# A graph layer's last stage: part of the sum moved from VectorE to accumulating DMAs, one maximum per tile shared with ScalarE, stores cut smaller

## The chip, the cores and the metric

The kernel runs on one core of a Trainium2 chip. Its engines are TensorE (PE), VectorE (DVE), ScalarE (ACT), GpSimd (POOL) and SyncE (SP); 16 DMA engines move data between DRAM and the core's SBUF. Each engine takes its instructions in program order and waits on semaphores. SP and ACT issue plain DMAs on queues q1 and q10, POOL issues its DMAs on q0. The metric is the device time of one execution in microseconds (us), lower is better. L12 is line 12 of the kernel before, unless the kernel after is named.

## What is computed

The input has 6250 nodes of 128 channels and 206250 edges (100000 in both directions and one loop for each node), sorted by their destination (dst). The reference, cut:

```
h = maximum(layernorm(x), 0)
feat = concat([h[dst], h[src] - h[dst]])
msg = feat @ W.T + b
out = segment_max(msg, dst)
return x + where(isfinite(out), out, 0)
```

With W = [W1 | W2] the message is (W1 - W2) h[dst] + b + W2 h[src]. The first two terms are the same for all edges of a dst. So the kernel computes, for each node, A + b with A = (W1 - W2) h, and B = W2 h; the result is x + A + b + max over the node's sources of B.

## The kernel before, in words

**Lanes.** Each of the 128 partitions (lanes) owns 49 consecutive dsts (the last lane owns 27), and their run of the sorted edges.

**Start (0 to about 170 us).** The kernel loads x, makes A + b and B on TensorE, stores B to a DRAM table `Bt`, and forms x + A + b in a DRAM table `XA`: first a DRAM to DRAM copy of x (L457), then five pairs of DMAs of POOL that add A + b to it, `G_.dma_start(..., accum_op=ALU.add)` (L508). VectorE also finds pairs of edges that fit a one-hot form (one edge at most for each source lane, place and dst) and those that don't, the rest.

**The dense part (the pairs).** 13 tiles t of 10 lanes each (8 in the last; 490 or 392 dst columns) run over 25 pairs of source groups i. For each of the 325 pairs, TensorE spreads an index (L782, PSUM tile `z`), ScalarE turns it into a one-hot `oh` (L783), TensorE multiplies B by it into PSUM tile `ps`, two banks of 490 columns (L831), and VectorE takes the running maximum into `acc2`, 980 columns a pair (L842). The first pair of a tile starts `acc2`: a copy for the first tile (L837), for the others the maximum of `ps` with the self edges that lie in `acc`, broadcast to both halves (L840). A tile's last pair folds both halves of `acc2` into `acc` (L849). ScalarE works two one-hots ahead. In tiles 1 and 2 it also counts list ends (L854), once for each pair.

**The stream.** The rest of the edges are 414 steps: step k has one row of `Bt` for each lane, gathered by an indirect DMA of POOL (L77) into the tile `rows`, which holds five groups of eight steps. VectorE takes a running maximum along the steps (L228, "stream step"), restarting it where a lane passes to a new dst. SP stores each finished group of 8 to a DRAM table `M` (L232). A 415th step joins runs that cross lanes. The steps are laid evenly over the pairs up to the 280th: `steps_until(k)` is 415 times (k - 1) over 278. On VectorE they stand between the maxima, so that a stream step which waits for its gather holds all the maxima behind it.

**The last gathers.** After the last store to `M`, POOL gathers 49 rows from `M`, the last one of each dst (L77, `HX<-M,last_e` x9 and `rows<-M,last_e` x40), one gather for each place in the lane.

**The tail.** The dsts of a lane go in six groups: places 0 to 8 (held in `HX`), then 9 to 16, 17 to 24, 25 to 32, 33 to 40 and 41 to 48 (in buffers of `rows`). In steps of four places, TensorE turns `acc` (L906), VectorE takes the maximum with the gathered rows (L907) and adds x + A + b (L911) from SBUF. These sums were loaded from `XA` ahead: 28 places into the tile `xa` when tile 6 starts, the other 21 into `T` in the last tile (`load_xa`, L814). Each group is stored when it is whole: lanes 0 to 111 by SP and the rest by ACT (L916).

The order on each engine is the order in which the program is written; nothing reschedules it.

Of the kernel before, what the change touches and what calls it, by code (L numbers as in the profile page):

```python
# [8 lines left out]
F32 = mybir.dt.float32  # L9
# [6 lines left out]
ALU = mybir.AluOpType  # L16
# [3 lines left out]
P = 128  # L20
# [8 lines left out]
LD = 49  # L29
# [3 lines left out]
NS = 414  # L33
# [3 lines left out]
U = 8  # L37
# [14 lines left out]
def gnn_kernel(tc, x, src, dst, W, b, out):  # L52
    nc = tc.nc
    N, C = x.shape
# [6 lines left out]
    NG = -(-NSX // U)  # L61
    GQ = 10
    LASTD = N - (P - 1) * LD
# [9 lines left out]
    def at(ap, offset, pattern):  # L73
        return bass.AP(tensor=ap.tensor, offset=ap.offset + offset, ap=pattern)
# [5 lines left out]
    with ExitStack() as ctx:  # L80
# [20 lines left out]
        with ExitStack() as body:  # L101
# [118 lines left out]
            def stream_step():  # L220
                k = state["ran"]
                if k == NSX:
                    return
                state["ran"] = k + 1
                i, j = divmod(k, U)
                G = Gt[i]
                if state["prev"] is not None:
                    V.scalar_tensor_tensor(G[:, j], state["prev"], slim[:, k:k + 1], G[:, j],  # L228
                                           op0=ALU.min, op1=ALU.max)
                state["prev"] = G[:, j]  # L230
                if j == U - 1 or k == NS:
                    nc.sync.dma_start(M_v[:, 1 + i * U:2 + i * U + j], G[:, :j + 1])  # L232

            def more_rows(to):
                while True:
# [506 lines left out]
            with ExitStack() as main:  # L742
# [61 lines left out]
                xa0 = fin1.tile([P, XD, C], F32, name="xa")  # L804
                xa1 = t3f[:, :(LD - XD) * C].rearrange("p (d c) -> p d c", c=C)

                def xa_of(d0, d1):
                    return xa0[:, d0:d1] if d1 <= XD else xa1[:, d0 - XD:d1 - XD]

                def load_xa(d0, d1):  # L810
                    for e, d2, d3, p0, p1 in ((nc.sync, d0, min(d1, LASTD), 0, 112), (A_, d0, min(d1, LASTD), 112, P),
                                              (nc.sync, max(d0, LASTD), d1, 0, 112), (A_, max(d0, LASTD), d1, 112, P - 1)):
                        if d2 < d3:
                            e.dma_start(xa_of(d2, d3)[p0:p1],  # L814
                                        at(XA, (p0 * LD + d2) * C, [[LD * C, p1 - p0], [1, (d3 - d2) * C]]))
# [4 lines left out]
                for k, (t, i) in enumerate(pairs):  # L820
# [13 lines left out]
                        self_edges(i)  # L834
                    more_rows(min(state["ran"] + 1, steps_until(k)))
                    if k == 0:
                        V.tensor_copy(a, ps[:, :, :n])  # L837
                    elif i == 0:
                        o = acc[:, c0:c0 + n].rearrange("c (o n) -> c o n", o=1).to_broadcast([P, 2, n])
                        V.tensor_tensor(a, ps[:, :, :n], o, ALU.max)  # L840
                    else:
                        V.tensor_tensor(a, a, ps[:, :, :n], ALU.max)  # L842
                    more_rows(steps_until(k))
                    oh = nxt
                    if k == Q // 2 - 1:
                        V.tensor_tensor(acc[:, c0:c0 + n], acc[:, c0:c0 + n], acc2[:, 0, :n], ALU.max)
                        V.tensor_tensor(acc[:, c0:c0 + n], acc[:, c0:c0 + n], acc2[:, 1, :n], ALU.max)
                    elif i == Q - 2:
                        V.tensor_tensor(acc[:, c0:c0 + n], acc2[:, 0, :n], acc2[:, 1, :n], ALU.max)  # L849
# [49 lines left out]
                V.tensor_copy(bad, bsum)  # L899
                acc_v = acc[:, :P * LD].rearrange("c (p d) -> c d p", d=LD)  # L900
                for R, (d0, d1) in zip(Rg, groups):
                    for j0 in range(d0, d1, 4):
                        j1 = min(j0 + 4, d1)
                        p = ps_f.tile([P, 4, P], F32, name="pf")
                        for j in range(j0, j1):
                            T_.transpose(p[:, j - j0], acc_v[:, j], ident)  # L906
                        V.tensor_tensor(R[:, j0 - d0:j1 - d0], R[:, j0 - d0:j1 - d0], p[:, :j1 - j0], ALU.max)  # L907
# [5 lines left out]
                    for e, d2, d3, p0, p1 in ((nc.sync, d0, min(d1, LASTD), 0, 112), (A_, d0, min(d1, LASTD), 112, P),  # L913
                                              (nc.sync, max(d0, LASTD), d1, 0, 112), (A_, max(d0, LASTD), d1, 112, P - 1)):
                        if d2 < d3:
                            e.dma_start(at(out, (p0 * LD + d2) * C, [[LD * C, p1 - p0], [1, (d3 - d2) * C]]),  # L916
                                        R[p0:p1, d2 - d0:d3 - d0])
                mid.close()


# [72 lines left out]
```

## Time and profile before

| | us |
|---|---|
| three runs: median (lowest, highest) | 790.54 (787.14, 792.31) |
| the profiled execution | 786.79 |
| its span, first to last instruction | 784.6 |
| VectorE busy | 724.9 (92%) |
| TensorE busy | 652.1 (83%) |
| ScalarE busy | 527.9 (67%) |
| GpSimd busy | 497.4 (63%) |

The tiles of the dense part take about 46 us each from 227 to 690 us, tile 11 ends at 732 us and tile 12 at 760 us; the tail is what follows. A row of a timeline has the start in us, the duration, the engine (SPq and ACTq are DMA issues), the line, the operation, what it writes <- what it reads, how many instructions were merged, and in brackets how long the engine sat idle before it and what ended the idle time. A row of windows has the stretch and its length, then busy us and number of instructions of PE, PEld (weight loads), DVE, ACT and POOL, the granted TensorE clock, the mean busy share of the DMA engines and GB/s. A row of a DMA queue has packets, MB, and the time of its packets as a share of 16 engines over the window.

### The profile page before, as it was taken

The numbers are of one execution on the slowest core, as the hardware profiler recorded it, in microseconds if no ns is written. First come the engines' busy times: TensorE is split into PE (matmuls) and PEld (weight loads), VectorE is DVE, ScalarE is ACT, GpSimd is POOL, SyncE is SP. The second block draws the span as 40 slices with busy tenths as digits, with TensorE's granted clock in tenths as the row PEclk, the third lists the DMA queues.
The fourth block names the chain that finished last, engine by engine and source line by source line (L and its number), as shares of the span: only waits on it lengthen the run. The fifth ranks groups of instructions, "written<-read, shape, count | busy, mean of one in ns | idle before, by whom it ended". The sixth has DMA issues, their size and how long they took to land. (4 is left out here: it accounts for less than half of the span.)

```text
span 784.6 us, 11914 instructions
## 1 busy us (share of the span) xinstructions
PE 652.1 (83%) x3571; PEld 421.7 (54%) x3571; DVE 724.9 (92%) x1329; ACT 527.9 (67%) x1212; POOL 497.4 (63%) x533
## 2 busy tenths in 40 slices
PE   1499776369888998699999998999999899898992
PEld 0254566348765555456555555655555555555661
DVE  5898999779799998999999999999999999997986
ACT  2659598337789999567576666657666665757740
POOL 5300012577777777777777767777777777747770
PEclk9799999559999999899999999999999999999996
DMA  3735264312334233333333373333333333324225
GB/s 87 212 89 209 37 131 96 88 48 81 105 89 117 80 104 105 103 102 109 105 103 105 105 188 110 106 104 104 103 107 102 103 105 105 104 84 111 62 57 169
DMA packets 77153, 83.05 MB, mean 106 GB/s; under 512 B 11585, under 2 KB 66213, under 8 KB 76677
## 3 DMA queue, kind: packets, MB, share of 16 engines
q1 hardware_dynamic: 60284, 45.40, 20.2%
q0 software_dynamic: 16096, 36.02, 17.1%
q10 hardware_dynamic: 700, 0.78, 0.6%
q8 instruction: 30, 0.49, 0.2%
q14 instruction: 43, 0.35, 0.1%
HBM read 44.41 MB, written 40.90 MB: 109 GB/s over the span
## 5 line engine op out<-in xcount | busy, mean ns | idle before, releaser
L77 POOL DMA_INDIRECT rows<-Bt,lists x414 | 416.6, 1006 | 135.2 <-DMA rows<-Bt,lists 44.5
L783 ACT ACTIVATE oh<-z 126x490 fp32r<-126x490 f32 (+1 forms) x650 | 336.9, 576 | 159.0 <-PE z L782 149.6
L831 PE MATMUL ps<-oh,Bp 126*128 126x490 f32 (+1 forms) x1300 | 389.1, 422 | 23.8 <-DVE acc L842 17.8
L842 DVE TENSOR_TENSOR acc<-acc,ps 128x980 f32<-128x980 f32 (+1 forms) x312 | 359.2, 1151 | 24.1 <-PE ps L831 19.4
L831 PEld LDWEIGHTS ps<-oh,Bp 126*128 126x128 f32 x1300 | 234.8, 193 | 147.1 <-DVE acc L842 90.5
L782 PE MATMUL z<-Vb,Sel 128*128 128x490 f16 (+1 forms) x650 | 195.0, 378 | 14.7 <-ACT oh L783 8.5
L228 DVE SCALAR_TENSOR_TENSOR rows<-rows,lists 128x128 f32<-128x128 f32 x414 | 142.1, 343 | 1.3 <-DMA rows<-Bt,lists 0.3
L191 PEld LDWEIGHTS <-HX 128*128 128x128 bf16 x896 | 68.1, 159 | 53.7 <-issue 36.7
L191 PE MATMUL pv<-HX 128*128 128x28 bf16 (+1 forms) x826 | 73.8, 232 | 16.2 <-ACT Vb L201 16.2
L782 PEld LDWEIGHTS <-Sel 128*128 128x128 f16 x650 | 43.2, 104 | 56.2 <-issue 54.6
L508 POOL DMA_DIRECT2D XA<-HX x10 | 9.9, 1215 | 95.4 <-issue 69.4
L168 DVE TENSOR_TENSOR HX<-T,IQ 128x700 bf16<-128x700 bf16 x128 | 65.3, 514 | 0.0
L560 PE MATMUL dup<-rows,identb 128*128 128x512 bf16 (+1 forms) x176 | 41.5, 376 | 14.9 <-DVE rows L569 13.6
L77 POOL DMA_INDIRECT rows<-M,last_e x40 | 37.7, 943 | 12.2 <-issue 7.0
L560 PEld LDWEIGHTS <-identb 128*128 128x128 bf16 x176 | 18.0, 102 | 36.8 <-issue 23.0
L854 ACT ACTIVATE dump<-lists,nbias 128x512 bf16<-128x512 f32 x50 | 37.6, 752 | 0.1
L499 PE MATMUL pm<-whi,lhl 128*125 128x256 f32 x100 | 25.4, 286 | 0.0
L499 PE MATMUL pm<-wlo,lhl 128*125 128x256 f32 x100 | 25.4, 286 | 0.0
L569 DVE TENSOR_TENSOR rows<-KA,KB 128x1792 bf16<-128x1792 int16 x22 | 23.9, 1085 | 0.9 <-PE dup L560 0.9
L476 ACT ACTIVATE rows<-HX,nmr,rstd 125x128 f32<-125x128 f32 x50 | 22.8, 523 | 2.5 <-DVE rows L421 2.5
L175 DVE TENSOR_TENSOR HX<-HX,T 128x392 bf16<-128x392 bf16 x64 | 23.2, 363 | 0.3
L569 DVE TENSOR_TENSOR rows<-KA 128x1792 bf16<-128x1792 int16 x21 | 22.7, 1082 | 0.6 <-PE dup L560 0.6
(264 smaller groups left out, 548.8 us busy)
## 6 DMA issues: line engine op xcount, KB each, us to landing
M<-rows SPq DMA_DIRECT2D x51, 512.0 KB
rows<-Bt,lists POOLq DMA_INDIRECT x414
HX<-in_x SPq DMA_DIRECT2D x5, 560.0 KB
Bt<-acc SPq DMA_DIRECT2D x5, 560.0 KB
XA<-HX POOLq DMA_DIRECT2D x5, 560.0 KB
out_x<-rows SPq DMA_DIRECT2D x4, 448.0 KB
xa<-XA SPq DMA_DIRECT2D x1, 1512.0 KB
T<-XA SPq DMA_DIRECT2D x1, 1176.0 KB
```

The costliest lines, as they stand in the source:

```text
L77: G_.indirect_dma_start(out=o, out_offset=None, in_=table, in_offset=bass.IndirectOffsetOnAxis(ap=idx, axis=0))
L168: V.tensor_tensor(oh, over(TQ, z - a), iq, ALU.is_equal)
L191: T_.matmul(o2[:, :, lo:lo + w], OHQ[:, :, i], OHD[:, :, :, i], start=False, stop=True, skip_group_check=True)
L228: V.scalar_tensor_tensor(G[:, j], state["prev"], slim[:, k:k + 1], G[:, j], op0=ALU.min, op1=ALU.max)
L499: T_.matmul(st["pm"][:L, j], a, w, start=False, stop=True, skip_group_check=True)
L560: T_.matmul(dup[:, c0:c1], m, e[:, c0:c1], start=first, stop=last)
L569: V.tensor_tensor(e, KA[:, 64:], i1, ALU.is_equal)
L782: T_.matmul(z[:, :n], Sel[:, Q - 1 - i - j], Vb[t % 2][:, :n], start=True, stop=True)
L783: A_.activation(oh[:, :n], z[:L + 1, :n], AF.Relu)
L831: T_.matmul(ps[:, j, :n], Bp[:, e, i + j], oh[j][:, :n], start=e == 0, stop=e == 1)
L842: V.tensor_tensor(a, a, ps[:, :, :n], ALU.max)
L854: A_.activation(dump, sdl, AF.Sign, scale=2.0, bias=nbias[:, c:c + 1], accum_out=ends[:, c:c + 1])
```

## The change

Five edits:

1. The first pair of a tile: in the first tile ScalarE makes the copy of both halves; in the other twelve, ScalarE copies the second half of `ps` and VectorE takes the maximum with `acc` for the first half alone.
2. The last group of the stream (7 steps): a store of five steps goes out after the fifth, and the last store has two steps in place of seven.
3. Places 0 to 24 (`SUM` = 25) take x + A + b in the output: when tile 7 starts, SP copies these places from `XA` to the output (one DRAM to DRAM DMA, 128 x 3200 elements). In the tail VectorE only takes their maximum, and POOL adds it to the output, one accumulating DMA for each of the three groups.
4. `xa` is loaded for places 25 to 27 alone.
5. The other 24 places are stored after each step of four places, and the last four in two steps of two.

```diff
+                if i == NG - 1 and j == (NS % U) - 2:
+                    nc.sync.dma_start(M_v[:, 1 + i * U:2 + i * U + j], G[:, :j + 1])
+                elif k == NS:
+                    j0 = (NS % U) - 1
                 if j == U - 1 or k == NS:
-                    nc.sync.dma_start(M_v[:, 1 + i * U:2 + i * U + j], G[:, :j + 1])
+                    nc.sync.dma_start(M_v[:, 1 + i * U + j0:2 + i * U + j], G[:, j0:j + 1])
...
+                SUM = groups[2][1]
...
                     if k == 0:
-                        V.tensor_copy(a, ps[:, :, :n])
+                        A_.copy(a, ps[:, :, :n])
                     elif i == 0:
-                        o = acc[:, c0:c0 + n].rearrange("c (o n) -> c o n", o=1).to_broadcast([P, 2, n])
-                        V.tensor_tensor(a, ps[:, :, :n], o, ALU.max)
+                        A_.copy(acc2[:, 1, :n], ps[:, 1, :n])
+                        V.tensor_tensor(acc2[:, 0, :n], ps[:, 0, :n], acc[:, c0:c0 + n], ALU.max)
...
+                    if i == 0 and t == len(tiles) // 2 + 1:
+                        w = [[LD * C, P], [1, SUM * C]]
+                        nc.sync.dma_start(at(out, 0, w), at(XA, 0, w))
                     if i == 0 and t in (len(tiles) // 2, len(tiles) - 1):
-                        load_xa(*((0, XD) if t < len(tiles) - 1 else (XD, LD)))
+                        load_xa(*((SUM, XD) if t < len(tiles) - 1 else (XD, LD)))
...
                 for R, (d0, d1) in zip(Rg, groups):
-                    for j0 in range(d0, d1, 4):
-                        j1 = min(j0 + 4, d1)
+                    cuts = list(range(d0, d1, 4)) + [d1]
+                    if d1 == LD:
+                        cuts.insert(-1, d1 - 2)
+                    for j0, j1 in zip(cuts, cuts[1:]):
                         p = ps_f.tile([P, 4, P], F32, name="pf")
                         for j in range(j0, j1):
                             T_.transpose(p[:, j - j0], acc_v[:, j], ident)
                         V.tensor_tensor(R[:, j0 - d0:j1 - d0], R[:, j0 - d0:j1 - d0], p[:, :j1 - j0], ALU.max)
+                        if d1 <= SUM:
+                            continue
                         ...
-                    for e, d2, d3, p0, p1 in ((nc.sync, d0, min(d1, LASTD), 0, 112), ...
+                        for e, d2, d3, p0, p1 in ((nc.sync, j0, min(j1, LASTD), 0, 112), ...
...
+                    if d1 <= SUM:
+                        G_.dma_start(at(out, d0 * C, [[LD * C, P], [1, (d1 - d0) * C]]), R[:, :d1 - d0],
+                                     accum_op=ALU.add)
```

On POOL, at the end of the program before: the gathers of the stream, the gather that joins runs, the 49 last gathers, and then the program's end (`bad` is a flag for inputs that the plan can't hold).

```order
L77 DMA rows<-Bt,lists 128x128 x414
L77 DMA rows<-M,lists 128x128
L77 DMA HX<-M,last_e 128x128 x9
L77 DMA rows<-M,last_e 128x128 x40
L922 TENSOR_LOAD bad
```

The same place in the program after (its lines are later by 6 to 19 in this part; L935 is the accumulating DMA of groups 0 to 2):

```order
L77 DMA rows<-Bt,lists 128x128 x414
L77 DMA rows<-M,lists 128x128
L77 DMA HX<-M,last_e 128x128 x9
L77 DMA rows<-M,last_e 128x128 x40
L935 DMA out_x<-HX 128x1152
L935 DMA out_x<-rows 128x1024 x2
L941 TENSOR_LOAD bad
```

All three accumulating DMAs stand behind the last of the 49 gathers.

On SP, from the stream's stores to the last load of `XA`, before:

```order
L232 DMA M<-rows 128x8x128 x27
L814 DMA xa<-XA 112x3456
L814 DMA xa<-XA 112x128
L232 DMA M<-rows 128x8x128 x24
L232 DMA M<-rows 128x7x128
L814 DMA T_85<-XA 112x2688
```

After (L238 and L234 are the stores to `M`, L823 the loads, L861 the copy to the output):

```order
L238 DMA M<-rows 128x8x128 x27
L823 DMA xa<-XA 112x256
L823 DMA xa<-XA 112x128
L238 DMA M<-rows 128x8x128 x5
L861 DMA out_x<-XA 128x3200
L238 DMA M<-rows 128x8x128 x19
L234 DMA M<-rows 128x5x128
L238 DMA M<-rows 128x2x128
L823 DMA T_85<-XA 112x2688
```

The load of `xa` shrinks to three places, the copy to the output comes five groups later on the same queue, and the stream's last store is cut in two.

On VectorE, the end of the program before, its last three steps of four places:

```order
L907 TENSOR_TENSOR rows<-rows,pf 128x512
L911 TENSOR_TENSOR rows<-rows,T_85 127x512
L907 TENSOR_TENSOR rows<-rows,pf 128x512
L911 TENSOR_TENSOR rows<-rows,T_85 127x512
L907 TENSOR_TENSOR rows<-rows,pf 128x512
L911 TENSOR_TENSOR rows<-rows,T_85 127x512
```

The start of VectorE's tail after (L921 is the maximum):

```order
L921 TENSOR_TENSOR HX<-HX,pf 128x512 x2
L921 TENSOR_TENSOR HX<-HX,pf 128x128
L921 TENSOR_TENSOR rows<-rows,pf 128x512 x5
L927 TENSOR_TENSOR rows<-rows,xa 128x256
L927 TENSOR_TENSOR rows<-rows,xa 127x128
L927 TENSOR_TENSOR rows<-rows,T_85 127x128
```

For the first 25 places the seven additions between the maxima are gone (the fifth maximum of the row x5 is that of places 25 to 28); from place 25 on a maximum and its additions alternate as before.

More of the change, by code (lines that the diff above doesn't have):

```diff
@@ L912, in gnn_kernel @@
                                                     ALU.add)
[L913 to L917, printed above, removed]
+                        for e, d2, d3, p0, p1 in ((nc.sync, j0, min(j1, LASTD), 0, 112), (A_, j0, min(j1, LASTD), 112, P),
+                                                  (nc.sync, max(j0, LASTD), j1, 0, 112), (A_, max(j0, LASTD), j1, 112, P - 1)):
+                            if d2 < d3:
+                                e.dma_start(at(out, (p0 * LD + d2) * C, [[LD * C, p1 - p0], [1, (d3 - d2) * C]]),
+                                            R[p0:p1, d2 - d0:d3 - d0])
+                    if d1 <= SUM:
+                        G_.dma_start(at(out, d0 * C, [[LD * C, P], [1, (d1 - d0) * C]]), R[:, :d1 - d0],
+                                     accum_op=ALU.add)
                 mid.close()
```

6 lines of the change are left out of this document (4 added, 2 removed).

## The prediction

> **What bounds the kernel now.** I read the page first, then windows by tile, the waits of VectorE, the timeline at both ends of the stream, and the DMA view of the tail. From the page, the engines and the gathers:
>
> ```profile
> PE 652.1 (83%) x3571; PEld 421.7 (54%) x3571; DVE 724.9 (92%) x1329; ACT 527.9 (67%) x1212; POOL 497.4 (63%) x533
> L77 POOL DMA_INDIRECT rows<-Bt,lists x414 | 416.6, 1006 | 135.2 <-DMA rows<-Bt,lists 44.5
> ```
>
> VectorE seems to be the bound, and in a middle tile (window view) it is busy for 45.75 of 46 us:
>
> ```profile
> 412.00:458.00 46.00, 42.11 (x224) 25.28 (x223) 45.75 (x84) 30.91 (x63) 35.34 (x36) 1.00 0.36 101
> ```
>
> But look at POOL's 36 gathers there. One takes 0.94 us when nothing stretches it, and 0.30 us pass before the next. The page's row says that 414 of them are busy for 416.6 us and idle for 135.2 us; 414 x 0.30 is 124 us, and 7.06 of the rest is the wait before the first. So the gathers run back to back from 148.86 us to 694: POOL is full too, though its column says 63%. The timeline shows who is ahead. POOL, gathers number 0, 1, 403 and 414 (11 gathers, and 11 steps, stand between 403 and the end):
>
> ```profile
> 148.86 1.04 POOL L77 DMA_INDIRECT rows<-Bt,lists  x1 [7.06 <-DVE lists L671]
> 150.20 1.23 POOL L77 DMA_INDIRECT rows<-Bt,lists  x1 [0.30 <-issue]
> 679.95 1.23 POOL L77 DMA_INDIRECT rows<-Bt,lists  x1 [0.30 <-DVE acc L842]
> 693.97 1.06 POOL L77 DMA_INDIRECT rows<-M,lists  x1 [0.31 <-DVE HX L168]
> ```
>
> VectorE, the stream steps that use the last three of these, and step 412:
>
> ```profile
> 178.57 0.35 DVE L228 SCALAR_TENSOR_TENSOR rows<-rows,lists 128x128 f32<-128x128 f32 x1
> 684.36 0.35 DVE L228 SCALAR_TENSOR_TENSOR rows<-rows,lists 128x128 f32<-128x128 f32 x1 [0.33 <-DMA rows<-Bt,lists]
> 695.91 0.34 DVE L228 SCALAR_TENSOR_TENSOR rows<-rows,lists 128x128 f32<-128x128 f32 x1
> 698.61 0.34 DVE L228 SCALAR_TENSOR_TENSOR rows<-rows,lists 128x128 f32<-128x128 f32 x1
> ```
>
> A step follows its gather's start by 28.4 us at first, by 4.41 at number 403 and 4.64 at the last. At 403 VectorE waited 0.33 us for the data: 4.41 us is how long a gather takes to land there. So VectorE has used up the whole lead of the gathers just when the stream ends. What it saves before that point it will spend waiting for gathers. This is the main reading of my prediction.
>
> **The tail.** PE, VectorE, POOL and the last store (timeline), the tail's window, then the DMA queues of 740 to 785 us and the busy tenths of the DMA engines from 774 to 785 (40 slices of 0.275 us):
>
> ```profile
> 759.99 5.56 PE L906 MATMUL pf<-ident,acc 128*128 128x128 f32 x29 [0.39 <-DVE acc L849]
> 760.79 0.69 DVE L907 TENSOR_TENSOR HX<-HX,pf 128x512 f32<-128x512 f32 x1 [0.60 <-PE pf L906]
> 769.35 0.68 DVE L907 TENSOR_TENSOR rows<-rows,pf 128x512 f32<-128x512 f32 x1
> ...
> 763.98 0.94 POOL L77 DMA_INDIRECT rows<-M,last_e  x1 [0.30 <-issue]
> 777.56 0.32 SPq L916 DMA_DIRECT2D out_x<-rows  x1
> 759.40:779.00 19.60, 9.84 (x51) 7.53 (x51) 17.04 (x31) 0.00 (x0) 4.30 (x5) 0.73 0.58 169
> q1 hardware_dynamic: 896, 2.81, 18.9%
> q10 hardware_dynamic: 218, 0.39, 5.0%
> ...
> DMA  9310009986976223999587510000000000000000
> ```
>
> VectorE sets the tail: it works from 760.79 to 777.5, busy for 17.04 of 19.6 us, the last store goes out at 777.56, the DMA engines fall idle at 780.4 (slice 23), and 4.2 us of closing work end the span at 784.6. All stores together took (18.9% + 5.0%) x 45 = 10.8 us of all 16 engines for 3.2 MB, so DMA has room today (0.58 busy in the window).
>
> **Edit 1, the first pair.** A whole maximum occupies VectorE for 1.09 us from its start to the next, one of 490 columns for 0.63 (first and third row, each with the start of the next):
>
> ```profile
> 462.88 1.17 DVE L840 TENSOR_TENSOR acc<-ps,acc 128x980 f32<-128x980 f32 x1
> 463.97 0.34 DVE L228 SCALAR_TENSOR_TENSOR rows<-rows,lists 128x128 f32<-128x128 f32 x1
> 461.72 0.70 DVE L849 TENSOR_TENSOR acc<-acc 128x490 f32<-128x490 f32 x1
> 462.35 0.35 DVE L172 TENSOR_TENSOR HX<-T,IW 128x392 bf16<-128x392 bf16 x1
> 463.67 1.05 ACT L783 ACTIVATE oh<-z 126x490 fp32r<-126x490 f32 x2 [0.81 <-PE z L782]
> 273.00:320.00 47.00, 42.19 (x221) 25.98 (x219) 44.70 (x83) 45.26 (x111) 36.33 (x36) 0.96 0.38 107
> 732.00:759.40 27.40, 25.86 (x142) 18.32 (x142) 24.87 (x27) 20.38 (x46) 20.69 (x23) 1.00 0.22 59
> ```
>
> So 0.46 to 0.5 us saved per tile. ScalarE's copy has no row; its nearest is the one-hot of the same 490 columns out of PSUM, half of 1.05, 0.5 us. It fits into the 0.81 us in which ScalarE waits there. Queued behind it are the one-hots of the pair after the next, which have that slack. In tiles 1 and 2 ScalarE is full (45.26 of 47 us), so there the copy costs what VectorE gains, but the gathers' lead of some 30 us covers that. The first tile's copy gains nothing: VectorE waits for `ps` around it. In tiles 3 to 11 VectorE saves 9 x 0.5 = 4.5 us, all before the stream's end, and of this only what the gathers allow arrives: number 403 lands at 684.36 as before, and of the 14.25 us of VectorE's work from there to the last step tile 11's first pair saves 0.5. The stream's end gains **0.5 us** of 4.5. Tile 12 starts behind the stream; TensorE is even fuller there (25.86 of 27.4 us, VectorE 24.87), so I count half of 0.5, **0.25**.
>
> **Edits 3 and 4, the loads.** The only hole in POOL's gathers, and the load of `xa` that made it (SP's row), with the DMA engines full (1.03 in the window):
>
> ```profile
> 457.01 1.56 SPq L814 DMA_DIRECT2D xa<-XA  x2
> 469.05 0.94 POOL L77 DMA_INDIRECT rows<-Bt,lists  x1 [2.63 <-DVE rows L228]
> 464.00:468.00 4.00, 3.38 (x13) 1.78 (x14) 4.00 (x10) 2.27 (x6) 1.89 (x2) 1.00 1.03 183
> 66.00:70.00 4.00, 3.66 (x17) 1.53 (x17) 4.00 (x5) 3.71 (x20) 0.00 (x0) 1.00 0.60 248
> ```
>
> 2.63 - 0.30 = 2.3 us lost on POOL, and as POOL is full, lost at the end. The load shrinks from 28 places to 3, but a copy of 25 places (1.64 MB) runs in tile 7. The last row is the same kind of copy (x to `XA`): it kept the engines at 0.60. POOL wins 2.3 us if the copy makes no hole, and loses 2.3 or so if its hole is twice as deep. Between them I take half of the old hole, a gain of **1.2 us**. The copy also stands ahead of 19 stores to `M` on SP's queue; a store that lands late holds POOL only when its buffer is due again, four groups or some 40 us later, so I price that at nothing; without that cover it would be the copy's length, some 8 us. The stream then ends 0.5 + 1.2 = 1.7 us earlier.
>
> **Edit 2, the cut store.** POOL waited for the last store to `M`, issued at 699.0 (first row):
>
> ```profile
> L232 SPq DMA_DIRECT2D M<-rows x52: 359/360/382, 186.5 to 699.0; - x52
> 702.75 0.94 POOL L77 DMA_INDIRECT HX<-M,last_e  x1 [7.72 <-issue]
> DMA  0000799700000050040140130005004099699998
> ```
>
> The last row, 698 to 716 us in slices of 0.45, shows its 448 KB moving in four slices, 1.8 us. Two steps of seven need 0.5, if the first five have gone by then (they leave after step 412, 2.7 us ahead): **1.3 us**; at worst nothing. With it the last gather ends at 764.92 - 1.7 - 1.3 = 761.9.
>
> **Edits 3 and 5, the tail.** Seven additions go from VectorE's path. But TensorE turns a place in 5.56/29 = 0.19 us, so the eighth maximum, the first with additions, begins 25 x 0.19 = 4.8 us after the first instead of 8.6 (769.35): VectorE's path gains 3.8 us. What comes late instead is the DMA work. POOL can issue the first accumulating DMA only behind its last gather, at 762.2, and needs about 1.2 us for it (mean of L508 below): data flow from 763.4. Their price comes from `XA`'s own. In 96 to 110 us one such pair ran beside a plain store of the same 0.64 MB (DMA slices of 0.35 us, then the plain queue and POOL's); last, POOL's issues of them:
>
> ```profile
> DMA  0000000799799999499999954000000000000000
> q1 hardware_dynamic: 154, 0.64, 14.6%
> q0 software_dynamic: 160, 0.64, 28.3%
> ...
> L508 POOL DMA_DIRECT2D XA<-HX x10 | 9.9, 1215 | 95.4 <-issue 69.4
> ```
>
> Of all 16 engines the plain store takes 2.04 us, the accumulating one 3.96, and the slices show both one after the other, 6 us: they add up. 25 places are 1.64 MB: 10.1 us. The other 24 places are 24/49 of 10.8, 5.3 us. That is 15.4 us of full DMA from 763.4 on: **778.8**, where it was 780.4. VectorE (last store at 777.56 - 3.8 - 1.95 = 771.8) no longer decides.
>
> The Trainium skill (DMA: Bandwidth & Descriptors, Anatomy of one DMA — SWDGE) fits a POOL DMA as 2.0 us and bytes over 436 GB/s. By that the three would move in 3.8 us, an estimate, and VectorE's path would stay the bound, as in rival B below. The trace disagrees for accumulating ones (3.96 us for 0.64 MB).
>
> **Sum.** 780.4 - 778.8 = 1.6 us off the span of 784.6. The profiled execution, 786.79, lies 3.75 us below the median; I take the same 1.6 off the median: **788.9 us**.
>
> **Rivals.** A, the gathers don't hold VectorE back (they land sooner than at 403): then 4.5 + 0.25 arrive. POOL's chain gains 4.5 + 1.3, DMA ends at 776.0: -4.4, 786.1 us. For it: number 403 was stretched (1.23 us where 0.94 is usual). Against it stands the wait at 684.36. B, accumulating DMAs hide among the stores, so that VectorE's path ends the tail: 771.8 + 2.8 (777.56 to 780.4), -5.8, 784.7 us. For it: today's tail leaves the engines at 0.58 on average. Against it: the sum of 2.04 and 3.96 above. A and B together: VectorE's last store at 777.56 - 3.8 - 4.75 = 769.0, the end -8.6, 781.9 us. C, slower: read-and-add in DRAM beside stores to the same tensor costs more than beside `Bt`'s store. It decides from 1.6 us more, 11.7 in place of 10.1; at twice 10.1 the end is +8.5, 799.0 us. For it: the stores now have runs of 1 to 2 KB in place of 4 KB, and all DMAs end in one pile. Against it: `XA`'s DMAs agree among themselves. D, nothing moves: ScalarE's copy comes late and VectorE waits as long as it saved; the tail then gives the 1.6 less 0.5, 789.4 us.
>
> **How the numbers follow.** Forecast 0.40, A 0.10, B 0.12, A and B 0.15, C 0.19, D 0.04. A measurement of this kernel can tell about 1% (7.9 us) from no change. Faster by over 1%: A with B, and 0.05 from the lower edges of A and B, 0.20. Slower by over 1%: C from 1.9 times on, 0.15. Within: 0.65. The range takes in A with B and C's milder part: 781.5 to 795. The forecast's own range, from the copy's hole (2.3 either way) and edit 2 at nothing, is 786 to 792.
>
> **What would show it.** Right: several waits of L228 for gathers between 600 and 700 us; the last gather of the stream within 2 us of 694; the DMA engines full from about 763 us, after VectorE's last maximum too. Wrong: no waits of L228 and a stream end 4 us earlier (A); idle DMA engines between stores, with the last store at the end (B); over 4.6 us for 0.64 MB of accumulating DMA (C); waits of L851 for ScalarE's copy (D).

## The result: 1.0 us slower, and the profile after

The changed kernel took 790.62 us (median of 22 runs, 787.93 to 793.06), the kernel before, beside it, 789.63 (22 runs, 787.14 to 793.01): ratio 1.0015, 95% interval 1.0003 to 1.0028. A second comparison gave 0.9996 (0.9977 to 1.0015). So: no gain, and perhaps a loss of 0.1%. The forecast was 1.6 us less. The profiled execution took 792.8 us, its span is 791.1.

The page of the changed kernel, engines and gathers; then VectorE's waits from 170 to 765 us (total, times, longest):

```profile
PE 650.1 (82%) x3566; PEld 424.6 (54%) x3571; DVE 714.2 (90%) x1323; ACT 534.6 (68%) x1225; POOL 507.9 (64%) x536
L77 POOL DMA_INDIRECT rows<-Bt,lists x414 | 422.2, 1020 | 133.3 <-DMA rows<-Bt,lists 44.8
```

```profile
DVE acc L851 <- PE ps L840: 19.1, 22, 3.5
DVE rows L228 <- DMA rows<-Bt,lists: 5.9, 5, 2.7
...
DVE acc L849 <- ACT acc L848: 1.5, 3, 0.6
```

VectorE has 10.7 us less to do (724.9 before). But it now waits 5.9 us for gathers, where it waited 0.33. And the 414 gathers, whose number and bytes did not change, keep POOL busy for 422.2 us in place of 416.6; their idle time fell by 1.9 (the wait before the first is 0.4 longer, the hole of tile 6 is gone). The stream in the timeline, POOL first (first gather, last of the stream, first and last of those behind it), then VectorE's last step:

```profile
151.12 1.04 POOL L77 DMA_INDIRECT rows<-Bt,lists  x1 [7.43 <-DVE lists L677]
699.53 1.01 POOL L77 DMA_INDIRECT rows<-M,lists  x1 [0.30 <-DVE HX L168]
707.24 1.19 POOL L77 DMA_INDIRECT HX<-M,last_e  x1 [6.70 <-DMA M<-rows]
769.96 0.96 POOL L77 DMA_INDIRECT rows<-M,last_e  x1 [0.30 <-issue]
704.11 0.34 DVE L228 SCALAR_TENSOR_TENSOR rows<-rows,lists 128x128 f32<-128x128 f32 x1
```

The tail: VectorE's first maximum and last operation, POOL's accumulating DMAs, the stores on SP, then the DMA engines from 766 to 792 (slices of 0.65 us) and their queues:

```profile
765.90 1.48 DVE L921 TENSOR_TENSOR HX<-HX,pf 128x512 f32<-128x512 f32 x3 [0.60 <-DMA rows<-M,last_e]
777.69 0.42 DVE L927 TENSOR_TENSOR rows<-rows,T 127x256 f32<-127x256 f32 x1
770.91 1.06 POOL L935 DMA_DIRECT2D out_x<-HX  x1
771.57 2.23 POOL L935 DMA_DIRECT2D out_x<-rows  x2
770.86 15.17 SPq L932 DMA_DIRECT2D out_x<-rows  x8
```

```profile
DMA  2212202037989999999999999999984621000000
...
q0 software_dynamic: 592, 1.97, 39.9%
q1 hardware_dynamic: 1024, 1.38, 17.4%
```

VectorE is through at 778.1, 13 us ahead of the end. The DMA engines are full from 771.8 to 786: they set the end, from POOL's last gather on. That part of the forecast holds.

**Where the time went.** The first gather of a program starts between 148.2 and 151.2 us in the profiles, so I compare three pieces, each from rows of the timeline like those above: the first gather's start to the last step's end ("stream"), from there to the end of the last of POOL's gathers ("gathers"), and from there to the span's end ("tail"). The last two columns show where VectorE stood: from its first maximum of the tail to its last operation, and to the end.

```
kernel                        stream   gathers  tail     VectorE  to end
before (the profile above)    550.09   65.97    19.68    16.74    23.81
before, once more (same)      550.71   65.98    21.00    16.75    23.68
forecast of the change        548.4    64.7     21.1
change (the profile above)    553.33   66.47    20.18    12.21    25.20
change, once more (after2)    550.59   66.40    19.96    12.20    24.96
change, other places (wide)   551.04   66.46    20.05    12.20    25.05
edit 1 alone (first)          551.21   66.61    20.06    16.72    23.62
edit 2 alone (cut)            551.00   66.06    21.06    16.75    23.69
edits 3, 4, 5 alone (tail)    552.31   66.31    21.93    12.21    24.81
```

The tail came out within 1.2 us of the forecast. The stream was to become 1.7 us shorter and is not shorter in any of the three; the gathers behind it were to take 1.3 us less and take 0.5 more. The experiments ask why.

### The profile page after: what moved, and what is told of

It is laid out like the page before. It is cut to its first block, busy times and chain, and to the rows that moved or that the text cites. A ratio compares the mean times of both kernels' runs of the same rounds, so it can differ in the third digit from the quotient of the medians.

```text
span 791.1 us, 11917 instructions
## 1 busy us (share of the span) xinstructions
PE 650.1 (82%) x3566; PEld 424.6 (54%) x3571; DVE 714.2 (90%) x1323; ACT 534.6 (68%) x1225; POOL 507.9 (64%) x536
## 4 chain that ended last, share of the span: by engine, by line
DVE 35%; PE 18%; ACT 15%; issue 15%; DMA 10%; POOL 1%; SPq 0%; DVEq 0%; POOLq 0%; ACTq 0%
DVE acc L851 14%; PE ps L840 9%; DVE rows L228 7%; DMA rows<-Bt,lists 7%; ACT oh L789 7%; PE z L788 4%; ACT dump L866 4%; DVE acc L632 3%; PE pv L191 2%; DVE acc L631 1%; ACT Vb L201 1%; ACT Vsq L200 1%; DVE rows L575 1%; PE z L797 1%; DVE HX L168 1%
## 5 line engine op out<-in xcount | busy, mean ns | idle before, releaser
L77 POOL DMA_INDIRECT rows<-Bt,lists x414 | 422.2, 1020 | 133.3 <-DMA rows<-Bt,lists 44.8
L840 PEld LDWEIGHTS ps<-oh,Bp 126*128 126x128 f32 x1300 | 237.3, 194 | 146.6 <-DVE acc L851 93.1
L228 DVE SCALAR_TENSOR_TENSOR rows<-rows,lists 128x128 f32<-128x128 f32 x414 | 143.1, 346 | 7.1 <-DMA rows<-Bt,lists 5.9
L168 DVE TENSOR_TENSOR HX<-T,IQ 128x700 bf16<-128x700 bf16 x128 | 65.6, 517 | 0.0
L77 POOL DMA_INDIRECT rows<-M,last_e x40 | 38.2, 955 | 12.2 <-issue 6.4
L175 DVE TENSOR_TENSOR HX<-HX,T 128x392 bf16<-128x392 bf16 x64 | 23.3, 364 | 0.3
```

Source lines behind the costliest of these rows:

```text
L77: G_.indirect_dma_start(out=o, out_offset=None, in_=table, in_offset=bass.IndirectOffsetOnAxis(ap=idx, axis=0))
L168: V.tensor_tensor(oh, over(TQ, z - a), iq, ALU.is_equal)
L840: T_.matmul(ps[:, j, :n], Bp[:, e, i + j], oh[j][:, :n], start=e == 0, stop=e == 1)
```

## Experiments: one edit at a time

All times are medians; "ratio" is that to the kernel before on the same chip. The edits are those of the change's diff.

**same** (the kernel before, unchanged) shows what the comparison can tell. 

> The kernel before, unchanged, for the spread between two sets of runs and for a second profile. Ratio 1.000 within 0.2%. Theory P (POOL's gathers set the time up to the tail, so their pace sets a run's time): a profile with a longer time than 786.8 us has longer gathers, about 0.94 us to 0.95 us at the 25th percentile for 5 us of time. Theory N (the two profiles differ by something else): the gather's duration does not follow the time.

 Measured: 787.92 us, ratio 1.0007 (0.9988 to 1.0026). Its profile is 3.4 us longer than that of before, and its usual (median) gather takes 944 ns, 945 before: theory N.

**first** (edit 1 alone: the two `A_.copy` lines and the half maximum). 

> Edit 1 alone on the kernel before. Theory P (VectorE's lead is used up at the end of the stream): -0.5 to -1 us, with waits of stream steps for gathers between 600 and 700 us. Rival V (VectorE is the bound, what it saves arrives): -4.5 us or more. Rival S (ScalarE's copy comes late and costs): +1 us or more, with waits of the pair's maximum for the copy.

 Measured: 788.13, ratio 1.0006 (0.9985 to 1.0027): of the 4.5 us that VectorE saves nothing arrives. Its waits and its gathers:

```profile
DVE rows L228 <- DMA rows<-Bt,lists: 7.8, 10, 2.6
```

```profile
L77 POOL DMA_INDIRECT rows<-Bt,lists x414 | 419.5, 1013 | 134.0 <-issue 42.4 <-DVE rows L228 32.6 <-DMA rows<-Bt,lists 21.0
```

VectorE now waits ten times for gathers, 7.8 us, more than it saved. And the gathers take 2.9 us longer than before, though no edit touches them.

**cut** (edit 2 alone: the last store to `M` in two parts). 

> Edit 2 alone on the kernel before (last store of the stream in 5 + 2 steps). VectorE sets the tail of the kernel before and the last gathers have 5 us of slack there, so 0 (within 0.5 us), though POOL's last gathers begin 1.0 us sooner after the store. If the last gathers bound the tail: -1 us.

 Measured: 789.22, ratio 1.0024 (1.0006 to 1.0043): slower if anything.

**tail** (edits 3, 4 and 5 alone). 

> Edits 3, 4 and 5 alone on the kernel before (accumulating DMAs, copy to the output in tile 7, small stores). By the prediction's terms: no hole in the gathers -1.2 to -2.3 us, and the tail's DMA work behind the last gather +1 us (20.2 us from the last gather to the end in place of 19.7, without the earlier gathers of edit 2): -1 us. Rival C (accumulating DMAs cost more than the forecast's 10.1 us): +2 us or more, and over 16 us of full DMA in the tail.

 Measured: 789.95, ratio 1.0021 (0.9999 to 1.0042). POOL has no hole in tile 6 any more, but VectorE, as long as ever, is now the later of the two. POOL's last gather of the stream, and VectorE's last step:

```profile
694.37 0.97 POOL L77 DMA_INDIRECT rows<-M,lists  x1 [0.30 <-issue]
```

```profile
703.11 0.35 DVE L228 SCALAR_TENSOR_TENSOR rows<-rows,lists 128x128 f32<-128x128 f32 x1
```

The step follows 8.7 us behind the gather (4.64 before): what POOL won became lead that nobody used. Behind the last gather this run needs 21.93 us (20.2 expected, 20.0 to 20.2 in the change); why was not found. Rival C asked for over 16 us of full DMA engines there; they are full for some 10.

**after2** (the change, unchanged). 

> The kernel after, unchanged, for a second profile on another occasion. Ratio to before 1.0015 within 0.2%. Theory P: its gathers' usual duration and the run's time move together, as between the two profiles at hand (0.94 us at 786.8 us, 0.95 us at 792.8 us), so with 0.94 us it takes 787 to 788 us.

 Measured: 788.81, ratio 0.9996 (0.9977 to 1.0015). Its profiled execution took 788.46 us with a usual gather of 952 ns, and that of same 790.2 with 944: the gather's duration does not set the time by itself.

## Experiments: who bounds the stream

**lead** takes 23 gathers out of the kernel before, so that POOL is ahead; **lead_first** adds edit 1 to that.

```
-                    else:
+                    elif not (i >= 6 and i % 2 == 0 and j == 3):
                         gather(G[:, j], Bt[:, :], ridx[:, k:k + 1])
```

> The kernel before with 23 of the 414 gathers of the stream left out (their steps take what an earlier gather left in the buffer), so that POOL is some 28 us ahead of VectorE again at the end. Theory P: VectorE has just met the gathers there, so -0.3 to -1 us. Rival V (VectorE alone is the bound): 0. If gathers already held VectorE back in a usual run: -3 us or more.

> The same with edit 1. Theory P: now what VectorE saves can arrive: 4 to 5 us less than with the gathers left out alone, though edit 1 by itself gives 0.5 to 1. Rival S (the copy on ScalarE eats the gain): as with the gathers left out alone, within 1 us.

Measured: lead 787.44, ratio 0.9982 (0.9964 to 0.9999); lead_first 783.23, ratio 0.9922 (0.9902 to 0.9943). Between them edit 1 is worth 4.2 us, nearly all of the 4.5 that the prediction counted (their intervals leave some 2 us either way); beside first's 1.0006 this shows that it is the gathers that withhold most of it. In the two profiles the stream itself is only 2.4 us shorter (549.66 and 547.22 us), and VectorE's waits for `ps` of TensorE grew from 19.7 to 27.0 us. The runs also show that VectorE is no less near: 23 gathers fewer, 29 us of POOL, gained 0.2%. The 391 gathers of lead, then of lead_first:

```profile
L77 POOL DMA_INDIRECT rows<-Bt,lists x391 | 394.5, 1009 | 134.5 <-issue 44.2
L77 POOL DMA_INDIRECT rows<-Bt,lists x391 | 397.6, 1017 | 134.5 <-issue 43.9
```

With edit 1 they take 3.1 us longer, though VectorE waits for none of them in either run.

**pool** adds POOL work, twelve fills, one ahead of a group.

```
                 G = rows[:, i % GB]
                 Gt[i] = G
+                if 6 <= i < 18:
+                    G_.memset(pad, 0.0)
```

> The kernel before with 12 added fills of a small tile on POOL, one ahead of each of 12 groups of gathers from group 6 on, some 0.5 us each with POOL's pause, 6 to 10 us in all. Theory P (POOL is full, and its lead is gone when the stream ends): the time grows by what POOL loses, +5 to +10 us. Rival V (VectorE is the bound, POOL has 28 us of lead): 0 within 1 us.

 Measured: 790.39, ratio 1.0013 (0.9996 to 1.003), less than expected. A fill in its place:

```profile
212.72 0.94 POOL L77 DMA_INDIRECT rows<-Bt,lists  x1 [0.30 <-DVE rows L231]
213.69 0.41 POOL L215 MEMSET pad<- 32x384 f16 x1
214.26 0.95 POOL L77 DMA_INDIRECT rows<-Bt,lists  x1 [0.16 <-DVE rows L231]
```

I had mis-sized the dose. From gather to gather 1.54 us pass with a fill and 1.25 without, so twelve cost 3.5 us; and the hole of tile 6, 2.63 before, shrank to 0.85. (In cut, which has no fills, it is 0.73, so that need not be the fills' doing.) What is left, 1.7 us, lies within the interval with 0. This run tells nothing apart.

**b_copy** adds the copy of edit 4 to the kernel before.

```
+                    if i == 0 and t == len(tiles) // 2 + 1:
+                        w = [[LD * C, P], [1, 25 * C]]
+                        nc.sync.dma_start(at(out, 0, w), at(XA, 0, w))
```

> The kernel before, and beside all it does the copy of 25 places from XA to the output in tile 7 (overwritten later by the stores). Prediction's step on the copy: half a hole, 1.2 us, ratio 1.0015, gathers held up around the copy. Rival: the copy hides, as the profile of the changed kernel shows no pause of POOL there, ratio 1.000. Question G: 952 ns a gather if the copy is the reason, else 945.

 Measured: 789.05, ratio 1.0000 (0.9982 to 1.0018). The copy leaves at 505.87, and POOL pauses only at the old place:

```profile
505.87 0.56 SPq L852 DMA_DIRECT2D out_x<-XA  x1
```

```profile
470.04 0.95 POOL L77 DMA_INDIRECT rows<-Bt,lists  x1 [2.44 <-DVE rows L228]
```

So the copy makes no hole. In tail and in the change, with the smaller load, the whole old one is gone: 2.3 us for POOL against the profile of before, where I took half. With the large load the hole is not the same in every run, 1.21 us in first, 0.73 in cut, 3.31 in small and none in padd25, of which 0.30 is the usual pause; so what edit 4 gives POOL differs between runs.

## Experiments: what lengthens the gathers

**wide, plain, nopool** are the change with, in this order, `xa` allocated as large as before; the three DMAs of L935 without `accum_op`; and the first 25 places stored by SP and ScalarE, with no DMA on POOL.

```
-                xa0 = fin1.tile([P, XD - SUM, C], F32, name="xa")        wide
+                xa0 = fin1.tile([P, XD, C], F32, name="xa")
-                                     accum_op=ALU.add)                   plain
-                        if d1 <= SUM:                                    nopool
-                            continue
...
-                                if a0 < a1:
+                                if a0 < a1 and d1 > SUM:
...
-                    if d1 <= SUM:
-                        G_.dma_start(...)
```

> The change whole, but the tile xa is allocated as large as before (28 places, 3 of them loaded), so that the one-hots and acc2 stand at the addresses they had before. Question G: 945 ns a gather and 3 us less than the changed kernel (ratio 0.998) if the place of the tiles in SBUF is the reason; 952 ns and the changed kernel's ratio (1.000 to 1.0015) if not.

> The change whole, but its three DMAs on POOL store plainly instead of adding (the first 25 places of a lane then hold the maxima alone, without x + A + b). Theory T (the tail is DMA-bound by accumulating DMAs at twice the price of plain ones): 10.1 us of DMA become 5.2 us, so 4.9 us less than the changed kernel (789.7 by all runs so far): about 785 us, ratio to before 0.995. Theory B (accumulating DMAs hide, something else ends the tail): no gain, ratio 1.000 to 1.0015. Question G, why every gather of the changed kernel takes 952 ns where the kernel before has 945: if the accumulating form on POOL's queue is the reason, gathers here take 945 and the stream gains another 3 us, ratio about 0.991; if not, 952.

> The change whole, but the first 25 places are stored plainly by SP and ScalarE's queues, four places at a time like the rest, and POOL issues no DMA behind its last gather (these places hold the maxima alone). Theory T: VectorE's path ends the tail, its last operation at 778.1 where the span ends at 791.1 in the changed kernel, 2.8 us to the last data, 4.2 to close: 6 us less, 783.5 us, ratio 0.992. Theory B: 0 to 1 us less, ratio 1.000. Question G: 945 ns a gather if POOL's three added DMAs are the reason (and 3 us more off), 952 if the smaller xa tile or the copy is.

Measured: wide 789.54, ratio 1.0005 (0.9989 to 1.0021); plain 786.11, 0.9963 (0.9945 to 0.9981); nopool 782.65, 0.9913 (0.9888 to 0.9939).

**b_pool3** puts three plain DMAs of 64 KB behind POOL's last gather in the kernel before.

```
+                for i in range(3):
+                    G_.dma_start(Dp[i * P:(i + 1) * P, :], ident)
```

> The kernel before, and three plain DMAs on POOL behind its last gather, 64 KB each, from a constant tile to a scratch tensor that nobody reads. Question G, whether their mere standing on POOL's queue slows each gather ahead of them: theory Q says yes, 952 to 955 ns a gather where the kernel before has 945, the stream some 3 us longer and the program's end with it, ratio 1.002 to 1.004. Rival: it is something else in the three DMAs of the changed kernel (their size, or that they write the output tensor), then 945 ns and ratio 1.000.

 Measured: 789.14, ratio 0.9998 (0.9980 to 1.0016). The gathers of b_pool3, then of nopool (shortest, median, longest in ns):

```profile
L77 POOL DMA_INDIRECT rows<-Bt,lists x414: 947/952/1938, 150.5 to 693.5; - x138
```

```profile
L77 POOL DMA_INDIRECT rows<-Bt,lists x414: 940/945/1940, 149.9 to 693.7; - x138
```

The median gather takes 951 to 955 ns in every kernel with further instructions on POOL behind its last gather (the change, wide, plain, tail, b_pool3, and three below) and 944 to 947 in every other one. But that alone costs no time: b_pool3's gathers together keep POOL busy for 416.6 us, just as before, as the gathers were stretched less. The sums of the 414 (the page's row of L77), one profile each, with the change's group the highest:

```
                       nothing behind on POOL               more behind on POOL
without edit 1         416.6 416.6 416.6 417.2 417.7 417.6  417.1 416.6 418.8 417.5
with edit 1            419.5 418.9                          422.2 420.0 421.0 421.5 420.4
```

(First row: before, same, cut, b_copy, small, cut_quiet; tail, b_pool3, padd25, padd17. Second: first, nopool; the change twice, wide, plain, nine.) So with edit 1 the gathers are some 2 us longer (3.1 in lead_first), and with POOL's DMAs too some 4: the step that the prediction did not have. The groups are single profiles that differ by up to 2.2 us among themselves.

**cut_quiet** asks what stretches a gather, at the place where edit 2 lost its gain. In cut the first of the last gathers began 2.73 us after the last step (3.80 before), 1.07 earlier as meant; but the 49 then took 63.33 us from first start to last end, 62.17 before. POOL in cut, then VectorE:

```profile
702.31 1.23 POOL L77 DMA_INDIRECT HX<-M,last_e  x1 [9.62 <-issue]
703.85 1.22 POOL L77 DMA_INDIRECT HX<-M,last_e  x1 [0.30 <-issue]
705.37 0.94 POOL L77 DMA_INDIRECT HX<-M,last_e  x1 [0.30 <-issue]
706.62 1.61 POOL L77 DMA_INDIRECT HX<-M,last_e  x1 [0.30 <-issue]
...
702.21 0.53 DVE L168 TENSOR_TENSOR HX<-T,IQ 128x700 bf16<-128x700 bf16 x1
703.72 0.53 DVE L168 TENSOR_TENSOR HX<-T,IQ 128x700 bf16<-128x700 bf16 x1
706.53 0.87 DVE L172 TENSOR_TENSOR HX<-T,IL 128x1372 bf16<-128x1372 bf16 x1
```

Each stretched gather begins while one of VectorE's one-hots runs, and the one between, 705.37, does not. cut_quiet is cut without the one-hots of the last pair of lanes.

```
+                if u == NLP - 1:
+                    z = SLOTS * SLOT
+                    return [lambda: A_.copy(hx16[:, z:z + 2 * w * NBLK], hx16[:, :2 * w * NBLK])] + [lambda: None] * 3
```

> Edit 2 alone, and VectorE's one-hots of the last pair of lanes (four operations, 698 to 712 us) left out: ScalarE copies older one-hots into their place, so part of the last tile's maxima is other than it should be. Question: why edit 2 brought nothing although its first last gather began 1.05 us sooner after the last step (2.73 us where it was 3.8). Theory V: the first nine last gathers are stretched by these one-hots of VectorE whenever one of them runs as a gather begins, and the earlier start put two more of them there. Then all nine take about 0.945 us here, the 49 gathers end 60.8 us after the first began (63.33 in the run cut, 62.17 before), 63.6 us after the last step (65.97 before). Rival: the gathers are stretched by the store to M or its rows still landing, then 1.2 us for most of the nine, as in cut, and 63 us for the 49.

 Measured: 787.77, ratio 1.0004 (0.9982 to 1.0025). POOL, then the one-hots of the pair before, which are still there:

```profile
701.60 1.23 POOL L77 DMA_INDIRECT HX<-M,last_e  x1 [6.92 <-issue]
703.14 1.22 POOL L77 DMA_INDIRECT HX<-M,last_e  x1 [0.30 <-issue]
704.66 0.94 POOL L77 DMA_INDIRECT HX<-M,last_e  x1 [0.30 <-issue]
705.91 0.94 POOL L77 DMA_INDIRECT HX<-M,last_e  x1 [0.30 <-issue]
...
701.49 0.53 DVE L168 TENSOR_TENSOR HX<-T,IQ 128x700 bf16<-128x700 bf16 x1
703.01 0.53 DVE L168 TENSOR_TENSOR HX<-T,IQ 128x700 bf16<-128x700 bf16 x1
```

Seven of the nine take 0.94 us; the two that still meet a one-hot at their start take 1.23 and 1.22. (I had overlooked that these two belong to the pair before, and expected nine.) The 49 take 61.45 us. That settles edit 2: the earlier start put two gathers more under one-hots, and they gave its microsecond back. The program gains nothing here either: without the accumulating DMAs its tail does not hang on POOL's last gather, which now ends 22.25 us before the span does (19.68 to 21.0 before).

## Experiments: the tail

plain and nopool answer the tail as well. Behind the last gather the change needs 20.0 to 20.2 us, plain 15.70, nopool 14.61. The DMA engines in plain, 766 to 786 us in slices of 0.5:

```profile
DMA  0503106979999999999989996847220000000000
```

With plain DMAs the end comes 4.3 to 4.5 us sooner, and nothing else in the program differs: that is what the accumulating form of 1.64 MB costs more than the plain one; the prediction had 10.1 - 5.2 = 4.9.

**nine** lets 9 places go by one accumulating DMA.

```
-                SUM = groups[2][1]
+                SUM = groups[0][1]
```

> The change with 9 places a lane going by one accumulating DMA instead of 25 by three. In the changed kernel the tail hangs on POOL's last gather and on what the DMA engines do behind it: 25.05 us from VectorE's first maximum of the tail to the end, 23.7 in the kernel before. With 9 places VectorE makes four more additions, 12.2 + 4 x 0.72 = 15.1 us to its last operation, then 6.0 as in the run small: 21.1 us. DMA: 3.6 us for 9 places from 6.2 us behind the first maximum on, and 8.8 for 40 plain ones, most of them in the time of VectorE's work: not the bound. Theory T (accumulating DMAs bind the tail): 3.9 us less than the changed kernel and 2.6 less than before in the tail, ratio about 0.996. Rival (the tail hangs on POOL's place in the order, whatever the amount): 25 us again, ratio 1.0015.

 Measured: 786.93, ratio 0.9994 (0.9975 to 1.0013). From VectorE's first maximum to the end 21.70 us pass, 25.0 to 25.2 in the change: 3.4 of the expected 3.9. Against the kernel before only 0.06% is left, and the interval holds 1. What the profile shows beside that: VectorE's first maximum of the tail came 63.03 us after the last step's end, 61.4 to 61.5 in the change, and TensorE's granted clock was 0.86 from 710 to 720 us there, 1.00 in the change (tile 12 is TensorE's). Other profiles go the same way (61.8 us at 1.00 in before, 63.3 at 0.85 in same). That this is the rest of the difference was not tested.

**small** has edit 5's cut stores alone, all additions on VectorE; **padd25** and **padd17** are small with the additions of the first 25 or 17 places done on POOL.

```
-                                    V.tensor_tensor(R[:p1, a0 - d0:a1 - d0], ...
+                        E_ = G_ if d1 <= 25 else V                      padd25 (17: padd17; V: small)
+                                    E_.tensor_tensor(R[:p1, a0 - d0:a1 - d0], ...
```

> The kernel before with edit 5's cutting of the stores alone: results leave four places at a time, the last two by themselves, all additions stay on VectorE, no DMA on POOL. From the profiles: from VectorE's first maximum of the tail to the end 23.7 us before, of which 6.95 behind VectorE's last operation; with the small last store that was 6.1 when all stores were plain. Expected 0.8 us less, ratio 0.999. Rival: the smaller runs of bytes in DRAM cost DMA time and eat it, ratio 1.000 or above.

> As the run small, and the additions of the first 25 places a lane are done by POOL as tensor operations in SBUF instead of VectorE, no accumulating DMA. VectorE's tail 12.2 us instead of 16.7. POOL is free 4.1 us behind VectorE's first maximum and has 6.25 additions of 512 columns; their price on POOL has no row yet. If one takes up to 1.3 us, VectorE's path ends the tail: 5.4 us less than before, ratio 0.993. At 2 us POOL ends 16.6 us behind the first maximum and the gain is 1 us, ratio 0.999. Rival: POOL's reads of SBUF hold up VectorE's own additions, ratio 1.000 or above. Question G: 945 ns a gather, as no DMA is added to POOL's queue.

> As padd25, with only the first 17 places added on POOL (4.25 additions of 512 columns); VectorE's tail 12.2 + 2 x 0.73 = 13.7 us. At up to 2.2 us an addition on POOL, VectorE's path ends the tail: 3.9 us less than before, ratio 0.995. Rival as for padd25.

Measured: small 788.55, ratio 0.9984 (0.9962 to 1.0006), from the first maximum to the end 22.91 us for 23.7, the 0.8 expected. padd25 789.08, 1.0006 (0.9988 to 1.0024); padd17 788.62, 0.9997 (0.9972 to 1.0022). In padd25 POOL's additions, and VectorE's own beside them:

```profile
L914 POOL TENSOR_TENSOR rows<-rows,xa x4: 1307/1512/1713, 768.5 to 772.7; 128x512 f32<-128x512 f32 x4
```

```profile
770.59 1.04 DVE L914 TENSOR_TENSOR rows<-rows,T 127x512 f32<-127x512 f32 x1
775.61 0.69 DVE L914 TENSOR_TENSOR rows<-rows,T 127x512 f32<-127x512 f32 x1
```

While POOL adds, VectorE's addition takes 1.04 us, afterwards 0.69, and POOL's own take 1.31 to 1.71 us, where its first two of this size took 1.08 and 1.09; its tail became 15.24 us, not 12.2. The rival was right.

No complete version beat both kernels by more than its interval; small came nearest. nopool shows what is there to be had, 0.9%, if the additions cost nothing.

## Why the prediction was wrong, step by step

**The main reading held.** POOL's gathers withhold what VectorE saves: edit 1 is worth nothing by itself and 4.2 us once POOL is ahead (first, lead, lead_first). The waits of L228 are there, 5 in the change and 10 in first. Rival A falls with that.

**The step that failed is the stream's sum.** It took a gather as a fixed 0.94 + 0.30 us and passed every microsecond that POOL saves on to the stream's end. The hole did go, 2.3 us and not the 1.2 I took. But in the change the gathers became 3.4 to 5.6 us longer (416.6 to 420.0 and 422.2), and -1.7 turned into +0.5 to +3.2 in the two profiles. Most of that is the usual gather: 952 and 955 ns in place of 945 make 2.9 and 4.1 us over 414. The gathers of the profiled change (shortest, median, longest in ns):

```profile
L77 POOL DMA_INDIRECT rows<-Bt,lists x414: 948/955/1937, 151.1 to 698.3; - x138
```

Why the usual gather is longer stays open (below). The rest is stretches. The prediction quoted their sign, gathers of 1.23 us among those of 0.94 (27 us of such stretches in the stream of before), and used it for rival A alone.

What stretches gathers can be counted in the timeline of before, by what VectorE was doing 0.12 us into each of POOL's gathers: under a one-hot (L168 to L175) 63 of 69 took 1.00 us or more, under a stream step (L228) 51 of 71, under a maximum that reads PSUM (L842) none of 269. The first two have both inputs in SBUF. (So has the fold, L849: 0 of 4.) In first, 99 gathers began under a step and 72 were stretched. It does not take a VectorE that waits for gathers: in lead_first, where it waits for none, 64 of 77 under a step were stretched, in lead 52 of 69. That the one-hots stretch gathers is shown (cut_quiet); that the steps do rests on counts alone, and why edit 1 puts more gathers under them, and why its share and that of POOL's later instructions add up, stays open. The Trainium skill (SBUF — State Buffer, Who interferes with whom) has the rule that a VectorE instruction with two SBUF inputs contends with a GpSimd instruction that reads SBUF; these counts and padd25's 1.04 us for 0.69 agree. The same section infers that `tensor_tensor` leaves descriptor generation alone; the gathers of cut and cut_quiet, 1.23 us with a one-hot and 0.94 without, are held up all the same, but whether in reading their indices or in making descriptors no run here tells.

**Edit 2** was to give 1.3 us. Its start came 1.0 us earlier; stretched gathers took that back (+1.2 in cut), and the longer gather, 955 for 945 ns over 49, another 0.5. Same mistake, smaller place.

**Edits 3 to 5, the tail.** The mechanism was right: DMA-bound behind the last gather, VectorE through long before. VectorE's path gained 4.53 us (3.8 forecast), the tail needed 20.0 to 20.2 us (21.1), the accumulating form 4.3 to 4.5 us more than plain (4.9). Rivals B and C fall: accumulating DMAs do not hide (plain gains 0.5%) and do not cost more than `XA`'s own had shown. D falls too: VectorE waited 1.5 us for ScalarE's copies in all. (Its longer wait in the first tile, 5.4 us for a one-hot, stands where it waited for `ps` and copied before.)

**The base.** I took 784.6 us as the span. same, unchanged, has 788.0. Of the 3.4 us, 1.45 lie ahead of the first gather, 0.6 in the stream and 1.3 behind the last step, where TensorE is the fullest engine and its granted clock was lower (windows of before, then of same; the clock is the number behind POOL's):

```profile
710.00:720.00 10.00, 8.50 (x40) 5.81 (x40) 6.29 (x7) 6.30 (x14) 7.85 (x8) 1.00 0.67 175
```

```profile
710.00:720.00 10.00, 8.43 (x33) 5.10 (x31) 6.07 (x8) 6.26 (x13) 7.87 (x8) 0.85 0.59 153
```

Against the mean of these two, the three profiles of the change (two and wide) have the stream 1.25 us longer, the gathers 0.5 longer and the tail 0.3 shorter, +1.4 in all, where the forecast had -1.7, -1.3 and +1.4. A sum of terms of 1 to 2 us against one profile has that much noise in it; only pieces that repeat, like the 23.6 to 23.8 us from VectorE's first maximum to the end, carry so small a term.

## What to carry to other kernels

When two engines are within one per cent of each other, shortening one buys lead, not time: give the other one slack on purpose (here 23 gathers less) and see what the saving is then worth. A duration that varies in the trace is not a constant of the sum: look at what the neighbour engine runs when the long ones start, since an edit that moves the start by a microsecond can change the duration by as much. Work handed to a queue that can only start behind the last step of another engine is not hidden, however idle the DMA engines were on average.

## What the runs showed of the hardware that I had not expected

- Of the gathers on POOL behind the stream in cut, those that began while VectorE ran a one-hot, with both inputs in SBUF, took 1.21 to 1.61 us in place of 0.94; the four whose one-hots were left out took 0.94 (cut_quiet). Beside a maximum with one input in PSUM none of 269 was stretched (before).
- The usual (median) gather of a program took 951 to 955 ns where one to three DMAs or five to seven additions stand behind the last gather on POOL, and 944 to 947 where not. Three small plain DMAs were enough for it (b_pool3); plain DMAs in place of accumulating ones (plain) or the old size of `xa` (wide) did not make it short again. Twelve fills between the gathers did not do it (946). Why is open.
- Three accumulating DMAs of 1.64 MB together from SBUF to DRAM put the end 4.3 to 4.5 us later than three plain ones (plain).
- An addition of 128x512 f32 took POOL 1.08 to 1.71 us beside VectorE's work, and VectorE 0.69 us alone and 1.04 to 1.35 beside POOL's additions (padd25).
